# Two expert lists instead of one, and the last stage of 18 images placed between the second lists

## The chip, the core and the metric

The kernel runs on one core of a Trainium2 chip. The core has five engines with an instruction queue each: TensorE (PE, matrix products and transposes, results in PSUM), VectorE (DVE), ScalarE (ACT), GpSimd (POOL, here also the engine that issues gathers and scatters) and SyncE (SP, which issues plain transfers). Each engine works through its queue in order and waits on semaphores for the others. The metric is the device time of one execution in microseconds, the median of several runs; the page and all views come from one profiled execution.

## The reference

Input: 32 images of 128 channels, 56 x 56 pixels, fp32; T = 100352 pixels, called tokens.

```
# layer 0
x   = depthwise_conv_7x7(input) + bias                  # per image and channel
x   = layernorm over the 128 channels of each token
logits = x @ Wg + bg                                    # 8 experts
two best experts per token, softmax over the two -> gates; priority = first gate
per expert: keep the CAP = 15680 tokens of highest priority (ties in token order)
y_e = gelu(x @ W1[e] + b1[e]) @ W2[e] + b2[e]           # 128 -> 512 -> 128
out = input + x + layer_scale * sum of gate * y_e over the kept experts
# layer 1, per image
pooled row and column means (weighted 7:3:1:1 over quarters) -> 1x1 conv to 8 channels
  -> h_swish -> two 1x1 convs -> sigmoids a_h, a_w
out = silu(batchnorm(conv_3x3(out * a_w * a_h)))
```

A token is in two experts' lists at most. What an expert keeps depends on all 32 images, because priorities are compared over all tokens.

## The kernel before

Four stages follow each other.

**Depthwise convolution and layer norm.** Two images at a time (a "pair", 49 columns of 128 tokens), the normalised rows and their gates go to `x_d` in memory, the rows alone to `acc_d`, and the first gate of each chosen token into `prio`, a table of 8 experts by 784 columns that stays on chip.

**Routing.** `Routing.steps(e, idx)` makes expert e's list in some fifty steps. 25 of them search the threshold by bisection: `count` (L411) counts on DVE how many entries of `prio[:, e, :]` lie over a bound and PE adds the counts over partitions (L412); three small DVE operations move the bound. Then ties at the threshold are ranked in token order (`keep`), the kept tokens get places by ten bit steps over 912 columns (L499 to L502), and two one-hot products turn places into row numbers `idx[0]` (for gathers) and `idx[1]` (for scatters). Expert 0's routing runs alone ahead of the experts; the other seven are dealt out as `steps` between the blocks of the experts in front of them.

**Experts.** A list is cut in blocks of 4 tiles of 128 tokens and the blocks in chunks (`CHUNKS`, 4, 7, 7, 7 and 6 blocks). For a block, POOL gathers 4 tiles of rows (L594), PE transposes them (L603), DVE copies them out of PSUM (L605), PE and ACT do the first product and the gelu (L613, L614), PE the second (L621), ACT adds the bias (L623), PE transposes back (L630), DVE multiplies by the gate (L640), and POOL scatters the 4 tiles into `acc_d`, adding in memory (L646). POOL gathers and scatters only blocks that hold tokens; PE, DVE and ACT compute every block of a chunk that holds any:

```
with tc.If(taken > CHUNKS[c] * BLK * P, preferred_fallthrough_block=True) as some:
    if c + 1 < NC_:
        gathers(e, c + 1, parts[e])
    compute(e, c, w, steps[c])
    if c + 1 < NC_:
        chunk(e, c + 1, w, steps)
left = [f for fs in steps[c:] for f in fs]
if left:
    with some.Else():
        for f in left:
            f()
```

So steps that were dealt to chunks that are not taken run by themselves, in the Else branch. In POOL's queue the order is: scatters of chunk c-1, gathers of chunk c+1, scatters of chunk c, and so on; the first chunk of the next expert is gathered ahead.

**Last stage.** After all scatters (a "fence" of small memsets on DVE makes the loads wait for them) the images come pair by pair: the accumulated rows are loaded in sevenths (`cxn`), transposed (`cpt`, L905) and added to the input (L907); PE and DVE pool them (L920 to L943); ACT makes the two sigmoids (L949, L950); DVE multiplies the image by both (L953, L954); POOL and ACT combine rows into six planes `v` of a transformed 3 x 3 convolution (L962 to L972); PE multiplies (L982: 6 planes by 3 taps, for each half of an image), DVE adds the products up (L988 to L992), ACT finishes with silu (L994) and stores. The products of a pair are issued a whole pair later than its gates; `v` has two buffers of a whole image, the products five PSUM buffers.

Instructions are written in program order; a scheduler then orders each engine's queue within a stretch between branches by its own estimate of durations.

Of the kernel before, what the change touches and what calls it, by code (L numbers as in the profile page):

```python
# [32 lines left out]
CHUNKS = (0, 4, 11, 18, 25, -(-ST // BLK))  # L33
NC_ = len(CHUNKS) - 1
CB = 7
RW = C + E
T1 = T + P
KB = 8
VB = 2
# [8 lines left out]
def moe_conv_then_coordatt_kernel(ctx: ExitStack, tc: tile.TileContext, a: dict, out: bass.AP):  # L48
# [12 lines left out]
    acc_d = dram.tile([T + ST * P + P, C], F32, name="acc_d")  # L61
# [101 lines left out]
    with ExitStack() as st:  # L163
# [24 lines left out]
        class Pair:  # L188
# [34 lines left out]
            def gates(self):  # L223
# [17 lines left out]
                nc.sync.dma_start(acc_d[rows, :].rearrange("(p j) c -> p j c", p=P), row[:, :, 0:C])  # L241
# [75 lines left out]
    with ExitStack() as st:  # L317
        rc = st.enter_context(tc.tile_pool(name="rc", bufs=1))
        sp = st.enter_context(tc.tile_pool(name="rts", bufs=2))
        rpp = st.enter_context(tc.tile_pool(name="rtp", bufs=1, space=PSUM))  # L320

        ones = rc.tile([P, P], F32, name="ones")
        nc.gpsimd.memset(ones, 1.0)
        ones_h = rc.tile([P, P], F16, name="ones_h")
        nc.gpsimd.memset(ones_h, 1.0)
        ones_t = rc.tile([P, NT], F16, name="ones_t")
        nc.gpsimd.memset(ones_t, 1.0)
        before = rc.tile([P, P], F32, name="before")
        nc.gpsimd.affine_select(out=before, in_=ones, compare_op=ALU.is_gt, fill=0.0,
                                base=0, pattern=[[1, P]], channel_multiplier=-1)  # L330
        before_h = rc.tile([P, P], F16, name="before_h")
        nc.vector.tensor_copy(before_h, before)
        behind_h = rc.tile([P, P], F16, name="behind_h")
        nc.gpsimd.affine_select(out=before, in_=ones, compare_op=ALU.is_gt, fill=0.0,
                                base=0, pattern=[[-1, P]], channel_multiplier=1)
        nc.vector.tensor_copy(behind_h, before)
        ii = rc.tile([P, ST], I32, name="ii")
        iota_h = rc.tile([P, ST], F32, name="iota_h")
        nc.gpsimd.iota(ii, pattern=[[1, ST]], base=0, channel_multiplier=0)
        nc.vector.tensor_copy(iota_h, ii)  # L340
        kk = rc.tile([P, KB], I32, name="kk")
        iota_k = rc.tile([P, KB], F32, name="iota_k")
        nc.gpsimd.iota(kk, pattern=[[1, KB]], base=0, channel_multiplier=0)
        nc.vector.tensor_copy(iota_k, kk)
        pk = rc.tile([P, KB], F32, name="pk")
        nc.gpsimd.iota(kk, pattern=[[P, KB]], base=0, channel_multiplier=1)
        nc.vector.tensor_copy(pk, kk)
        pcol = pk[:, 0:1]
        spare = rc.tile([P, ST], F32, name="spare")
        nc.vector.tensor_scalar(spare, iota_h, float(P), float(T), ALU.mult, ALU.add)  # L350
        nc.vector.tensor_scalar(spare, spare, pcol, None, ALU.add)
        to_come = rc.tile([1, NC_], F32, name="to_come")
        for c in range(NC_):
            nc.gpsimd.memset(to_come[:, c : c + 1], float(BLK * P * (1 - CHUNKS[c]) - 1))
        most = rc.tile([1, NC_], F32, name="most")
        for c in range(NC_):
            nc.gpsimd.memset(most[:, c : c + 1], float(BLK * P * (CHUNKS[c + 1] - CHUNKS[c] + 1) - 1))
        first = rc.tile([P, 1], F32, name="first")
        nc.vector.tensor_copy(first, spare[:, 0:1])
        shift = rc.tile([P, 1], F32, name="shift")  # L360
        nc.vector.tensor_scalar(shift, pcol, -float(P), None, ALU.add)

        junk = rc.tile([P, NT], F32, name="junk")

        class Routing:

            def __init__(self, n):  # L370
                t = lambda name, shape, dt: rc.tile(list(shape), dt, name=f"{name}_r{n}")
                self.cnt = t("cnt", [P, 1], F32)
                self.mid = t("mid", [P, 1], F32)
                self.enough = t("enough", [P, 1], F32)
                self.thr = t("thr", [P, 1], F32)
                self.room = t("room", [P, 1], F32)
                self.eq = t("eq", [P, NT], F16)
                self.run = t("run", [P, NT], F16)
                self.nth = t("nth", [P, NT], F32)
                self.keep = t("keep", [P, NT], F16)  # L380
                self.gone = t("gone", [P, NT], F16)
                self.n = t("n", [P, 1], F16)
                self.bi = t("bi", [P, 1], I32)
                self.lo = t("lo", [P, 1], I32)
                self.left = t("left", [1, NC_], F32)
                self.room_l = t("room_l", [P, 1], F32)
                self.h0 = t("h0", [P, 1], F32)
                self.v = t("v", [P, KB * P], U16)
                self.bit = t("bit", [P, P + NT], U16)
                self.dist = t("dist", [P, KB * P], F16)  # L390
                self.full = t("full", [P, KB * P], F16)
                self.hk = t("hk", [P, KB], F32)
                self.hot = t("hot", [P, 2, KB, ST], F16)
                self.q = t("q", [P, ST], F32)
                self.qi = t("qi", [P, ST], I32)
                self.a = t("a", [P, ST], F32)
                self.pair = t("pair", [P, ST], F32)
                self.ps = rpp.tile([P, 2, ST], F32, name=f"ps_r{n}")

            def steps(self, e, idx):  # L400

                r, out = self, []
                tot = r.ps[:, 0, 0:1]

                def step(f):
                    out.append(f)

                def count(op, scalar):  # L410
                    nc.vector.tensor_scalar(junk, prio[:, e, :], scalar, None, op, ALU.add, accum_out=r.cnt)  # L411
                    nc.tensor.matmul(tot, lhsT=ones, rhs=r.cnt, start=True, stop=True)  # L412

                for b in range(1, 25):

                    @step
                    def _(b=b):
                        if b == 1:  # L420
                            nc.vector.memset(r.thr, 0.5)
                        else:
                            nc.vector.tensor_scalar(r.enough, tot, float(CAP), 2.0 ** (1 - b), ALU.is_ge, ALU.mult)
                            nc.vector.tensor_tensor(r.thr, r.thr, r.enough, ALU.add)
                        nc.vector.tensor_scalar(r.mid, r.thr, 2.0**-b, None, ALU.add)
                        count(ALU.is_ge, r.mid)


                @step
                def _():  # L430
                    nc.vector.tensor_scalar(r.enough, tot, float(CAP), 2.0**-24, ALU.is_ge, ALU.mult)
                    nc.vector.tensor_tensor(r.thr, r.thr, r.enough, ALU.add)
                    count(ALU.is_gt, r.thr)

                by_pair = r.run.rearrange("p (i j) -> p i j", j=TPP)

                @step  # L440
                def _():
                    nc.vector.tensor_scalar(r.room, tot, -1.0, float(CAP) + 0.5, ALU.mult, ALU.add)
                    nc.vector.tensor_scalar(r.eq, prio[:, e, :], r.thr, None, ALU.is_equal)
                    nc.vector.tensor_tensor_scan(r.run, ones_t, r.eq, 0.0, ALU.mult, ALU.add)


                    pre = r.ps[:, 0, 0:NPAIR]
                    nc.tensor.matmul(pre, lhsT=before_h, rhs=by_pair[:, :, TPP - 1], start=True, stop=False)
                    nc.tensor.matmul(pre[:, 1:NPAIR], lhsT=behind_h, rhs=by_pair[:, 0 : NPAIR - 1, TPP - 1],
                                     start=False, stop=True)  # L450

                @step
                def _():
                    nc.vector.tensor_tensor(r.nth.rearrange("p (i j) -> p i j", j=TPP), by_pair,
                                            bc(r.ps[:, 0, 0:NPAIR].unsqueeze(2), [P, NPAIR, TPP]), ALU.add)

                @step
                def _():
                    nc.vector.scalar_tensor_tensor(r.keep, r.nth, r.room, r.eq, ALU.is_le, ALU.mult)

                @step
                def _():
                    nc.vector.scalar_tensor_tensor(r.keep, prio[:, e, :], r.thr, r.keep, ALU.is_gt, ALU.add)

                @step
                def _():

                    nc.vector.tensor_tensor_scan(r.gone, ones_t, r.keep, 0.0, ALU.add, ALU.subtract)
# [608 lines left out]
```

## Time and profile before

| | us |
|---|---|
| median of 3 runs (4669.65 to 4675.83) | 4672.91 |
| profiled execution | 4676.35 |
| its span, first to last instruction | 4674.5 |
| PE busy | 3662.5 (78%) |
| POOL busy | 2692.2 (58%) |
| DVE busy | 2173.8 (47%) |
| ACT busy | 1314.9 (28%) |

The shares are means over four stages with different limits, so they say little; the stages have to be read one by one. On the page, a group's line shows engine and operation, names and shapes, the number of instructions, busy time and mean duration in ns, then the idle time of that engine just before them and what ended it. "issue" means that nothing the profile shows was waited for. `PEclk` or "granted clock" is the share of TensorE's full clock.

### The profile page before, as it was taken

How to read it: one execution, taken by the hardware profiler on the slowest of the kernel's cores; microseconds unless marked ns; L12 is line 12 of the kernel's file. 1: busy time of each engine (PE TensorE's matmuls, PEld its weight loads, DVE VectorE, ACT ScalarE, POOL GpSimd, SP SyncE). 2: the span in 40 equal slices, each digit the busy share in tenths (PEclk: the TensorE clock that was granted, in tenths of full speed). 3: DMA queues.
4: the chain of work that ended last, by engine and by line, in shares of the span. 5: the costliest groups of instructions: out<-in, count | busy, mean ns of one | idle time of the engine just before them, and what ended most of it. 6: DMA issues, size and time to landing. Idle time of an engine off the chain costs nothing. (4 is left out here: it accounts for less than half of the span.)

```text
span 4674.5 us, 50118 instructions
## 1 busy us (share of the span) xinstructions
PE 3662.5 (78%) x17669; PEld 2031.1 (43%) x17669; DVE 2173.8 (47%) x4727; ACT 1314.9 (28%) x2555; POOL 2692.2 (58%) x1862
## 2 busy tenths in 40 slices
PE   9999989775167667767667756687582999999999
PEld 4444449775133333433333322333231555555555
DVE  1111117988757346654521101111013877787776
ACT  1111117554022222222223322232230333333333
POOL 1001003354068878678778766887785756565655
PEclk9999999877578878878778977888785999999999
DMA  9999987987322333323323332333335344344432
GB/s 155 176 176 176 176 177 255 343 314 275 123 43 37 42 55 36 42 43 40 44 44 43 43 46 44 44 42 42 46 41 126 136 151 151 123 156 151 154 124 74
DMA packets 866353, 526.90 MB, mean 113 GB/s; under 512 B 543880, under 2 KB 835488, under 8 KB 855648
## 3 DMA queue, kind: packets, MB, share of 16 engines
q1 hardware_dynamic: 504848, 327.79, 24.6%
q0 software_dynamic: 118720, 91.19, 14.9%
q10 hardware_dynamic: 242320, 102.85, 9.8%
q8 instruction: 155, 2.54, 0.2%
q14 instruction: 310, 2.54, 0.2%
HBM read 268.72 MB, written 252.97 MB: 112 GB/s over the span
## 5 line engine op out<-in xcount | busy, mean ns | idle before, releaser
L646 POOL DMA_INDIRECT acc_d<-yo,idx x676 | 1074.3, 1589 | 251.1 <-issue 198.7
L614 ACT ACTIVATE ht<-ph,bias 128x512 f32<-128x512 f32 (+1 forms) x700 | 477.9, 683 | 929.8 <-PE ph L613 928.1
L982 PE MATMUL pc<-v,wk 128*128 128x392 f32 x1920 | 696.9, 505 | 3.2 <-POOL v L967 3.2
L613 PE MATMUL ph<-fxt,w 128*128 128x512 f32 (+1 forms) x1400 | 683.1, 631 | 0.0
L137 PE MATMUL acc<-xt,band 56*64 56x424 f32 (+3 forms) x7168 | 668.9, 529 | 2.6 <-DMA xt<-in_x 2.6
L594 POOL DMA_INDIRECT xg_r<-x_d,idx x556 | 546.1, 982 | 175.6 <-issue 139.8
L621 PE MATMUL py<-ht,w 128*128 128x512 f32 (+1 forms) x1400 | 633.5, 596 | 5.8 <-POOL w L666 5.8
L982 PEld LDWEIGHTS pc<-v,wk 128*128 128x128 f32 x1920 | 344.9, 189 | 306.5 <-issue 94.4
L137 PEld LDWEIGHTS acc<-xt,band 56*64 56x64 f32 x7168 | 321.7, 133 | 349.2 <-issue 276.7
L605 DVE COPY fxt<-pt 128x512 f32<-128x512 f32 (+1 forms) x175 | 119.6, 683 | 748.6 <-PE pt L603 684.0
L603 PE MATMUL pt<-ident,xg_r 128*128 128x128 f32 (+1 forms) x568 | 125.6, 326 | 432.9 <-DMA xg_r<-x_d,idx 414.2
L962 POOL TENSOR_TENSOR d<-pad 128x3248 f32<-128x3248 f32 x32 | 228.2, 7132 | 406.4 <-DVE pad L954 406.4
L275 PE MATMUL lnps<-proj,lnyt 128*128 128x136 f32 x1568 | 361.7, 399 | 103.0 <-ACT sq L280 75.0
L275 PEld LDWEIGHTS lnps<-proj,lnyt 128*128 128x128 f32 x1568 | 349.7, 316 | 115.6 <-ACT sq L280 86.5
L125 POOL COPY band<-hk 56x392 f32<-56x392 f32 x128 | 65.3, 510 | 575.5 <-issue 527.5
L613 PEld LDWEIGHTS ph<-fxt,w 128*128 128x128 f32 x1400 | 273.0, 206 | 270.9 <-issue 262.2
L621 PEld LDWEIGHTS py<-ht,w 128*128 128x128 f32 x1400 | 258.4, 193 | 272.4 <-issue 263.9
L150 DVE TENSOR_SCALAR yt<-acc,dwb 128x448 f32<-128x448 f32 x128 | 87.5, 684 | 584.6 <-PE acc L137 337.0
L992 DVE SCALAR_TENSOR_TENSOR y<-pc,y 128x392 f32<-128x392 f32 x640 | 318.4, 557 | 32.3 <-PE pc L982 32.3
L623 ACT ACTIVATE fyt<-py,b 128x512 f32<-128x512 f32 (+1 forms) x175 | 119.6, 683 | 654.8 <-PE py L621 641.9
L603 PEld LDWEIGHTS pt<-ident,xg_r 128*128 128x128 f32 (+1 forms) x568 | 81.5, 163 | 505.9 <-DMA xg_r<-x_d,idx 369.0
L640 DVE TENSOR_TENSOR yo<-pb,xg_r 128x512 f32<-128x512 f32 (+2 forms) x147 | 98.3, 671 | 416.1 <-PE pb L630 363.3
(221 smaller groups left out, 4505.2 us busy)
## 6 DMA issues: line engine op xcount, KB each, us to landing
x_d<-xn SPq DMA_DIRECT2D x16, 3332.0 KB
xt<-in_x SPq DMA_DIRECT2D x128, 392.0 KB
y_d<-yt ACTq DMA_DIRECT2D x256, 196.0 KB
lnyt<-y_d SPq DMA_DIRECT2D x16, 3136.0 KB
acc_d<-xn SPq DMA_DIRECT2D x16, 3136.0 KB
x<-in_x SPq DMA_DIRECT2D x16, 3136.0 KB
cxn<-acc_d SPq DMA_DIRECT2D x112, 448.0 KB
out<-y ACTq DMA_DIRECT2D x64, 784.0 KB
```

The lines of the kernel that those rows point to most:

```text
L137: nc.tensor.matmul(acc[c][half * G : (half + 1) * G, :, lo:hi], lhsT=band[rows, dw, :], rhs=xt[rows, im, lo + s : hi + s], start=(n == 0), ...
L275: nc.tensor.matmul(ps[:, j, :], lhsT=yf[:, self.j0 + g + j, :], rhs=proj, start=True, stop=True)
L594: d = nc.gpsimd.indirect_dma_start(out=xg[0:n, k, :], out_offset=None, in_=x_d[:, :], in_offset=bass.IndirectOffsetOnAxis(ap=idx[0][0:n, t ...
L603: nc.tensor.transpose(pt[:, k * P : k * P + n], xg[0:n, k, 0:C], ident[0:n, 0:n])
L605: nc.vector.tensor_copy(xt[:, 0:N_], pt[:, 0:N_])
L613: nc.tensor.matmul(ph[:, 0:N_], lhsT=w[0][:, f * P : (f + 1) * P], rhs=xt[:, 0:N_], start=True, stop=True)
L614: nc.scalar.activation(ht[:, f, 0:N_], ph[:, 0:N_], AF.Gelu, bias=w[2][:, f : f + 1])
L621: nc.tensor.matmul(py[:, 0:N_], lhsT=w2[:, f, :], rhs=ht[:, f, 0:N_], start=(f == 0), stop=(f == NF - 1))
L646: d = nc.gpsimd.indirect_dma_start(out=acc_d[:, :], out_offset=bass.IndirectOffsetOnAxis(ap=idxs[e][1][0:n, t : t + 1], axis=0), in_=yo[0: ...
L962: nc.gpsimd.tensor_tensor(d, high, low, ALU.subtract)
L982: nc.tensor.matmul(m[k], lhsT=wk[k][:, dw, :], rhs=v[:, k, rows, dw : dw + W], start=(dw == 0), stop=(dw == 2))
L992: nc.vector.scalar_tensor_tensor(r[x], m[k], f, r[y_], ALU.mult, ALU.add)
```

## The change

The images are cut in two groups (`GROUPS`: pairs 0 to 8 and 9 to 15, so 18 and 14 images). Each expert has two lists, one per group; lists 0 to 7 are those of the first group, 8 to 15 those of the second. Each group has its own accumulator. All eight thresholds are searched ahead of everything, on all experts in two halves that take turns; `kept` then marks kept tokens over all 32 images, `listed` makes one group's list from them (at most 441 columns instead of 784). The routing of all 16 lists is dealt out among lists 0 to 7.

The last stage is cut into some twenty pieces per image (`slot`): seven `merge` (load, transpose, add, for 8 rows), `squeeze`, `pooled`, `attend` (sigmoids), `gate`, `combined` (the planes `v`, for half an image), `conv` (one or two planes' products and sums). The pieces of images 0 to 17 are dealt out as `steps` among lists 8 to 15; there `combined` runs on DVE alone. The 14 others follow after the last list, with `combined` on POOL and ACT as before. Buffers change: `xs` and `cx` (loads of 8 rows) have three, `pad` two, `v` one per half image, products two PSUM buffers beside the lists and five afterwards, borrowed from the experts' pools.

The scaling of W2 by the layer scale moves from POOL to DVE, chunks have 4, 6, 6, 6, 6 and 3 blocks, and weights are loaded once per list, so twice per expert.

```diff
-CHUNKS = (0, 4, 11, 18, 25, -(-ST // BLK))
-CB = 7
+CHUNKS = (0, 4, 10, 16, 22, 28, -(-ST // BLK))
+CB = 6
+GROUPS = ((0, 9), (9, NPAIR))
...
-    acc_d = dram.tile([T + ST * P + P, C], F32, name="acc_d")
+    acc_d = [dram.tile([T + ST * P + P, C], F32, name=f"acc{g}_d") for g in range(NG)]
...
+    def count(h, op, bound):
+        es = sides[h]
+        for e in range(es.start, es.stop):
+            nc.vector.tensor_scalar(junk, prio[:, e, :], bound[:, e : e + 1], None, op, ALU.add, accum_out=cnt[:, e : e + 1])
+        nc.tensor.matmul(tots[h], lhsT=ones, rhs=cnt[:, es], start=True, stop=True)
...
+    for b in range(1, 25):
+        for h in range(2):
+            if b > 1:
+                raised(h, 2.0 ** (1 - b))
+            nc.vector.tensor_scalar(mid[:, sides[h]], thr[:, sides[h]], 2.0**-b, None, ALU.add)
+            count(h, ALU.is_ge, mid)
...
-            nc.gpsimd.tensor_tensor(w2, w2, bc(ls_bc.unsqueeze(1), [P, NF, C]), ALU.mult)
+        nc.vector.tensor_tensor(w2, w2, bc(ls_bc.unsqueeze(1), [P, NF, C]), ALU.mult)
...
+    SHARES = (7, 9, 7, 2, 1, 1)
+    PIECES = (56, 48, 40, 40, 40, 40, 40, len(order))
+    for l in range(E):
+        w = one_list(l, w, dealt(some_routing(PIECES[l]), SHARES))
...
+    def merge(n, q):
+        k = (NM * n + q) % 3
+        pt = trp.tile([P, BLK * P], F32, tag="tr", name=f"cpt{n}_{q}")[:, 0 : BLK * MT]
+        for j in range(BLK):
+            nc.tensor.transpose(pt[:, j * MT : (j + 1) * MT], cxs[k][:, j, :], ident[0:MT, 0:MT])
+        nc.vector.scalar_tensor_tensor(pads[n % 2][:, 1 + q * MB : 1 + (q + 1) * MB, 1 : W + 1],
+                                       pt.rearrange("c (r w) -> c r w", w=W), beta_c, xss[k], ALU.add, ALU.add)
+        m = NM * n + q + 3
+        if m // NM in group_of and group_of[m // NM] == group_of[n]:
+            load(m // NM, m % NM)
...
+    def gate(n):
+        img = pads[n % 2][:, 1 : H + 1, 1 : W + 1]
+        nc.vector.tensor_tensor(img, img, bc(aw.unsqueeze(1), [C, H, W]), ALU.mult)
+        nc.vector.tensor_tensor(img, img, bc(ah.unsqueeze(2), [C, H, W]), ALU.mult)
+
+    def combined(n, ch, shared):
...
+        if shared:
+            nc.scalar.mul(t, low[:, :, 1:3, :], 4.0)
+            nc.gpsimd.tensor_tensor(d, high, low, ALU.subtract)
...
+        else:
+            stt = nc.vector.scalar_tensor_tensor
+            stt(t, low[:, :, 1:3, :], -4.0, high[:, :, 1:3, :], ALU.mult, ALU.add)
+            nc.vector.tensor_tensor(d, high, low, ALU.subtract)
+            nc.vector.tensor_tensor(v[:, 1], t[:, :, 1, :], t[:, :, 0, :], ALU.add)
...
+        out_ += [new(merge, n, 0), cv(0, 1, 2), old(combined, n - 1, 1, shared),
+                 new(merge, n, 1), cv(0, 3), new(merge, n, 2), cv(0, 4), new(merge, n, 3), cv(0, 0), cv(0, 5),
+                 new(squeeze, n, 0), new(merge, n, 4), cv(1, 1, 2), new(merge, n, 5), new(merge, n, 6), new(squeeze, n, 1),
+                 cv(1, 3), new(pooled, n), cv(1, 4), new(attend, n), cv(1, 0), cv(1, 5), new(gate, n),
+                 new(combined, n, 0, shared)]
...
+    few = {k: (pcp, "pc") for k in range(6)}
+    many = {1: (pcp, "pc"), 2: (pcp, "pc"), 3: (php, "ph"), 4: (php, "ph"), 0: (pyp, "py"), 5: (pcp, "pc")}
...
+    LSHARES = (8, 10, 6, 1, 1, 1)
+    for g in range(1, NG):
+        pieces = [f for n in range(2 * GROUPS[g - 1][0], 2 * GROUPS[g - 1][1]) for f in slot(n, False, few)]
+        at = [0] + [len(pieces) // (2 * E) + (len(pieces) - len(pieces) // (2 * E)) * e // (E - 1) for e in range(E)]
+        for e in range(E):
+            l = g * E + e
+            steps = dealt(pieces[at[e] : at[e + 1]], LSHARES if e else (0,) + LSHARES[1:])
...
+    scatters(len(lists) - 1, NC_ - 1)
+    fenced(yo_all[0] + yo_all[1])
+    for n in range(2 * GROUPS[-1][0], N + 1):
+        for f in slot(n, True, many):
+            f()
```

## The prediction

> **What bounds the kernel now.** I read the page first, then the stages by windows, then groups by shape, then the timeline where two stages meet. The page's dearest groups:
>
> ```profile
> span 4674.5 us, 50118 instructions
> ...
> L646 POOL DMA_INDIRECT acc_d<-yo,idx x676 | 1074.3, 1589 | 251.1 <-issue 198.7
> ...
> L982 PE MATMUL pc<-v,wk 128*128 128x392 f32 x1920 | 696.9, 505 | 3.2 <-POOL v L967 3.2
> ...
> L594 POOL DMA_INDIRECT xg_r<-x_d,idx x556 | 546.1, 982 | 175.6 <-issue 139.8
> ...
> L962 POOL TENSOR_TENSOR d<-pad 128x3248 f32<-128x3248 f32 x32 | 228.2, 7132 | 406.4 <-DVE pad L954 406.4
> ```
>
> A tile of 128 tokens costs POOL a scatter (1.59 us) and a gather (0.98), each with 0.3 us of issue before it. The scatters' idle is almost all "issue", so POOL waits for nobody there. The windows by stage (us, PE, PEld, DVE, ACT, POOL busy, granted clock, DMA share, GB/s):
>
> ```profile
> 1198.80:1301.90 103.10, 19.98 (x83) 17.28 (x83) 79.33 (x219) 0.00 (x0) 2.55 (x3) 0.50 0.18 62
> 1301.90:3553.00 2251.10, 1547.15 (x4734) 776.38 (x4734) 709.26 (x1783) 598.47 (x876) 1746.27 (x1363) 0.82 0.32 43
> 3553.00:3650.00 97.00, 49.69 (x231) 27.10 (x231) 69.49 (x107) 15.44 (x16) 47.98 (x26) 0.72 0.56 181
> 3650.00:4600.00 950.00, 946.47 (x3663) 500.85 (x3663) 752.89 (x1198) 325.63 (x316) 594.99 (x230) 1.00 0.41 140
> ```
>
> First the routing of expert 0, alone. Then the experts: 676 tile pairs in 2251 us, 3.33 us a pair, POOL the bound, PE idle 700 us. Then a start of 97 us, then the last stage, where PE is 99.6% busy at the full clock: 33.2 us an image (the timeline repeats every 33). Group rows by shape price the DVE parts, the timeline a block of 512 tokens on PE:
>
> ```profile
> L411 DVE TENSOR_SCALAR_CACHE_REDUCE junk<-prio,mid_r 128x784 f32<-128x784 f32 x192 | 196.9, 1025 | 3.8
> ...
> L954 DVE TENSOR_TENSOR pad<-x,ah 128x3136 f32<-128x3136 f32 x32 | 111.8, 3494 | 0.0
> ...
> L953 DVE TENSOR_TENSOR x<-x,aw 128x3136 f32<-128x3136 f32 x32 | 110.4, 3451 | 4.1 <-ACT aw L950 4.1
> ```
>
> ```profile
> 3483.27 3.60 PE L613 MATMUL ph<-fxt,w 128*128 128x512 f32 x8
> 3486.70 0.60 PE L630 MATMUL pb<-ident,fyt 128*128 128x128 f32 x4
> 3487.14 3.60 PE L621 MATMUL py<-ht,w 128*128 128x512 f32 x8
> 3490.57 0.58 PE L603 MATMUL pt<-ident,xg_r 128*128 128x128 f32 x3
> ```
>
> From 3483.27 to 3491.09: 7.82 us a block, undisturbed.
>
> **The work in the lists.** Counting kept tokens with the reference's routing on its inputs, experts 0 to 7 take 31, 15, 25, 31, 2, 4, 31, 31 blocks: 170, or 676 tiles, as the scatters show. PE computes whole chunks: 175. After the cut, images 0 to 17 take 18, 9, 14, 18, 1, 2, 31, 31 (124 blocks, 494 tiles; PE computes 140), the rest 13, 7, 11, 14, 1, 2, 0, 0 (48 blocks, 192 tiles; PE computes 74). Experts 6 and 7 have more tokens of first gate exactly 1.0 than places, and ties go in token order, so all they keep lies in the first 15 images. Two things follow: PE gets 39 blocks more (305 us of PE), and four of the eight second lists leave POOL next to nothing to do while over half of the image work is dealt to them.
>
> **Step 1, thresholds.** 25 counts for 8 experts: 200 on DVE, 1.08 us apart where the timeline has two in a row, plus 50 half steps of three small operations at 0.19 us: 216 + 28 = 244 us. The round over PE (0.76 us) hides behind the other half. Before, only expert 0's 25 rounds of 2.3 us stood here (57). The rest of its routing took 45 us at 784 and 912 columns; at 441 and 569 the ten bit steps shrink from 24 to 15, so 36. First gather at 1199 + 244 + 36 = 1479 instead of 1302. Nothing covers this: all of prio must exist and no list is ready. The 175 counts that leave the expert stage (about 290 us of DVE with their small operations) give nothing back, because DVE is 31% busy there.
>
> **Step 2, first lists.** 494 pairs at 3.33 us: 1645 (at the undisturbed pace of 1.25 + 1.86 us: 1536). Lists 4 and 5 need POOL for 13 and 27 us but carry 40 routing steps each, some 55 us of DVE: 40 us more, between 0 and 80. Gathering list 8's first chunk ahead: 20 us. PE ends 44 us before POOL does, as now (3510 against 3554). PE is free for the second lists at 1479 + 1645 + 40 + 20 - 44 = 3140. The yo memsets, the second accumulator and the scaling moved from POOL to DVE cost nothing here; the DVE's idle time hides them, otherwise 16 times 0.6 us.
>
> **Step 3, second lists beside 18 images.** PE owes 74 x 7.82 = 579 and 18 x 33.2 = 598; POOL owes only 192 x 3.33 = 639. So PE bounds it, and all of the last stage's PE work is still ahead. At the front, the fence memsets on DVE wait for list 7's last scatters; queued behind them are list 8's copies, for which PE waits. Four blocks (31 us) stand before, POOL needs some 44: with the constants' DMAs 25 us (0 to 60). SP now carries the weights behind image loads that wait for merges; they are needed a list later, so nothing, or a landing of 3 to 4 us a list if the loads stand still.
> Where a list ends early, its image pieces run alone. By the shares that is 19/27 of the pieces of lists 12 to 15 and some of the others: 8.3 images. There DVE now does the row combinations too: 24 passes at 0.49 (nine in 4.42 us in the timeline), 7 merges at 0.56 (two of 512 columns take 1.26), squeeze and pooling 3.3, gate 6.9, and 9744 elements at L953's 1.1 ns (10.7): 36.6 us, plus waits for products, 42 an image (33 if PE stayed the bound, 48 with POOL-like waits): 349. The other 9.7 images mix with the blocks: 322 + 579 = 901 us of PE. It works in order, with two PSUM buffers for products, two shared for transposes, one v a half, and products waiting for gate and combinations. I take 90% dense, between the 99.6% of the stage now and the 69% beside POOL: 1001. Sum 349 + 1001 + 25 = 1375, to 4515.
>
> **Step 4, the last 14 images.** Now an image's products run a whole pair behind its gate, so the 7 us gate and POOL's 20 us hide. In the built order of the changed kernel they run right behind: after an image's two sigmoid products come the next image's seven merges, then at once products that need v. In that loop: merges on DVE 2.4 us, gate 3.45, merge 0.6, gate 3.49 (9.9); POOL then d for half an image 3.57, t 1.54, one v 0.89, v1 0.82: the first product starts at 16.7. PE has 5 us of transposes and squeeze to fill that. Then 72 matmuls at 0.328 and the rest, 26 us. Loop 42.7. The same stall costs clock. Rows around an idle stretch of 11.5 us on PE:
>
> ```profile
> 1774.80:1777.10 2.30, 0.00 (x0) 0.00 (x0) 0.00 (x0) 0.68 (x1) 2.00 (x2) 1.00 0.54 54
> 1777.10:1786.30 9.20, 0.07 (x1) 0.07 (x1) 2.78 (x10) 0.00 (x0) 7.67 (x6) 0.50 0.39 34
> 1786.30:1790.70 4.40, 4.40 (x9) 2.23 (x10) 4.37 (x7) 0.91 (x2) 2.39 (x3) 0.50 0.18 17
> ```
>
> After 2.3 us idle the clock halves, and PE works 4.4 us before it returns: 2.2 us lost a stall. So 45 us an image, against 33.2: 14 x 45 = 630, and 46 for the last image's loop, products and store: 676.
> [...]
> [...]
>
> **Sum.** 3140 + 1375 + 676 = 5191, and 1.9 us that the profiled execution has around its span (4676.35 against 4674.5); it lies 3.4 above the median of the runs shown (4672.91): 5190 us, 11% slower. Ends: lists 3050 to 3200, second lists 1240 to 1500, last images 560 to 730. About 0.2% is what a measurement can tell from no change.
>
> **Rivals.** *Dense overlap (faster).* Pieces and blocks fill each other's waits, 33.2 us an image throughout, POOL at its undisturbed 3.11 us: 1479 + 1536 + 20 - 44 = 2991, then 579 + 598 + 465 + 25: 4658, and 4660 with the 1.9 around the span, 0.35% under the profiled execution. For it: a scheduler orders the pieces, and PE is 99.6% dense today. Against it: the built order of step 4. It decides while PE stalls for under 16 us in all, half a microsecond an image; beyond that the change is slower.
> *Loop half hidden.* If the merges and spare banks take most of the stall, 37 us an image last, 38 alone, 96% dense mixed, lists done at 3110: 3110 + 315 + 939 + 25 + 564 = 4953.
> *Cold PE.* If stalls of the mixed part also halve the clock again and again, as the 0.82 of the expert stage shows can be, 72% dense, 48 and 50 us an image, lists at 3170: 3170 + 398 + 1251 + 25 + 750 = 5594.
> *The split is not as counted.* The change may not empty lists 14 and 15: were ties at 1.0 not as in my count, experts 6 and 7 would leave 13 blocks each behind. Then 26 blocks of 13.3 us (346) leave the first lists and PE computes 24 more (188) in the second: near 5030.
>
> **How the numbers follow.** The sum above 64% (own range 5060 to 5330), half hidden 17%, another split 2%, cold 12%, dense 5%. Outside 4930 to 5430 lie most of the dense and cold cases and the low edge of the half hidden one, together under 20%. Faster by over 0.2% only in the dense case, 4%, no change 1%, slower 95%: the PE work behind step 2 alone is 1640 us, against 1121 now, and POOL gives back only 182 pairs.
>
> **What would show it.** Right: first gather near 1479; PE busy over 85% from about 3140 on while POOL falls to half; 42 to 48 us between sigmoids in the last 14 images with granted clock under 1.0. Wrong: a first gather before 1420, an image period under 38 at the end, second lists done within 1250 us, or POOL still dense after 3200.

## The result, and the profile after

The changed kernel takes 5324.56 us (median of 4, 5322.45 to 5325.98) against 4673.63 for the kernel before on the same chip: a ratio of 1.1393, 95% interval 1.1374 to 1.1413. The forecast was 5190 (4930 to 5430), so the sign and the range held; the time is 134 us above the forecast, and most of that sits in one term (step 2 below). The profiled execution has a span of 5320.7 us.

The groups of the page that answer to those shown of before:

```profile
span 5320.7 us, 54751 instructions
...
L662 POOL DMA_INDIRECT acc_d<-yo,idx x686 | 1137.3, 1658 | 600.7 <-issue 245.5
L1009 PE MATMUL pc<-v,wk 128*128 128x392 f32 x2304 | 870.3, 527 | 140.8 <-DVE v L995 67.1
...
L609 POOL DMA_INDIRECT xg_r<-x_d,idx x502 | 494.6, 985 | 254.5 <-issue 107.2
...
L609 POOL DMA_INDIRECT xg_f<-x_d,idx x184 | 192.4, 1046 | 311.8 <-DVE idx L581 235.3
```

686 scatters, as counted (494 + 192), at 1.66 us each against 1.59 for the 676 of before. What changed are the idle columns: the image products (L1009), which waited 3.2 us in the whole kernel before, now have 140.8 us of idle time before them, most of it for their row combinations (67.1 us for those on DVE, 54.9 for those on POOL), and the first gather waits 235.3 us for the thresholds and the first list. The stages by windows (us, PE, PEld, DVE, ACT, POOL busy, granted clock, DMA share, GB/s), cut where the first gather, list 8's first transpose and the end of the images beside the lists lie:

```profile
1198.80:1451.50 252.70, 33.73 (x129) 28.73 (x129) 248.83 (x644) 0.00 (x0) 5.70 (x13) 0.50 0.06 20
1451.50:3217.00 1765.50, 1248.88 (x3595) 571.55 (x3596) 514.93 (x1401) 480.35 (x701) 1300.48 (x1016) 0.83 0.29 42
3217.00:4626.00 1409.00, 1186.79 (x4135) 596.58 (x4133) 760.82 (x1217) 432.89 (x551) 546.95 (x403) 0.92 0.35 83
4626.00:5320.70 694.70, 549.93 (x1920) 286.19 (x1920) 376.65 (x632) 173.40 (x204) 313.81 (x232) 0.85 0.31 99
```

Row one is DVE alone (98% busy). Row two is POOL's stage, as in the kernel before. In row three PE is 84% busy and POOL falls to 39%: PE owes image work and blocks, and POOL is done with little. In row four nobody is the bound: PE 79%, DVE 54%, POOL 45%, and the clock at 0.85 where it was 1.00 before. That is the mark of a loop of waits. One of its periods, from the timeline, PE first, then DVE and POOL:

```profile
4855.37 0.38 PE L963 MATMUL pa<-z_t,wwt 8*128 8x56 f32 x2
...
4862.69 0.57 PE L929 MATMUL cpt<-ident,cx 112*128 112x112 f32 x4 [2.81 <-DMA cx<-acc_d]
...
4872.90 18.91 PE L1009 MATMUL pc<-v,wk 128*128 128x392 f32 x48 [3.12 <-POOL v L985]
...
4901.58 0.38 PE L963 MATMUL pa<-z_t,wwt 8*128 8x56 f32 x2
```

```profile
4858.37 3.42 DVE L969 TENSOR_TENSOR pad<-pad,aw 128x3136 f32<-128x3136 f32 x1
...
4862.30 3.42 DVE L970 TENSOR_TENSOR pad<-pad,ah 128x3136 f32<-128x3136 f32 x1
```

```profile
4865.86 3.65 POOL L981 TENSOR_TENSOR d_t<-pad 128x1624 f32<-128x1624 f32 x1 [24.57 <-DVE pad L970]
4869.44 1.64 POOL L984 TENSOR_TENSOR t_t<-pad,t_t 128x812 f32<-128x812 f32 x1
```

From one image's sigmoid product to the next it is 46.2 us, in every period. After the sigmoid come the gate (two passes of 3.42 us with merges between), then POOL's d and t, and only then the first product: 17.1 us after the sigmoid product's end, and PE has only transposes and squeeze products for that time, some 8 us of work. PE's waits in the last images, from 4640 to 5275:

```profile
PE cpt L929 <- DMA cx<-acc_d: 56.3, 29, 3.2
PE pc L1009 <- POOL v L985: 40.2, 13, 3.1
```

(us in total, times, longest.) More is put down to the image loads than to the combinations, but the waits for loads lie within those 17.1 us, in which DVE goes on from the merges to the gate and POOL from d to v without a pause, so the loads do not set when the products start. The clock in this stretch (same columns as in the stages):

```profile
4862.00:4864.00 2.00, 1.31 (x6) 0.53 (x6) 2.00 (x2) 0.00 (x0) 0.00 (x0) 1.00 1.04 410
4864.00:4866.00 2.00, 0.12 (x2) 0.10 (x2) 2.00 (x2) 0.19 (x1) 0.14 (x1) 0.56 1.08 343
...
4876.00:4878.00 2.00, 2.00 (x4) 1.01 (x4) 0.00 (x0) 0.00 (x0) 2.00 (x2) 0.53 0.00 0
4878.00:4880.00 2.00, 2.00 (x7) 1.13 (x6) 0.00 (x0) 0.00 (x0) 2.00 (x2) 1.00 0.00 0
```

It halves near 4864 and returns near 4878. The products that start at 4872.90 run at half rate for 5.0 us of that, 2.5 us lost in this period. Over the 13 periods the products begin with 2.9 to 6.0 us at half rate, 4.4 in the mean: 2.2 us lost a period, as forecast.

### The profile page after: what moved, and what is told of

It is laid out like the page before. It is cut to its first block, busy times and chain, and to the rows that moved or that the text cites. A ratio compares the mean times of both kernels' runs of the same rounds, so it can differ in the third digit from the quotient of the medians.

```text
span 5320.7 us, 54751 instructions
## 1 busy us (share of the span) xinstructions
PE 4046.4 (76%) x18517; PEld 2152.9 (40%) x18517; DVE 2424.3 (46%) x5246; ACT 1443.3 (27%) x2785; POOL 2439.1 (46%) x1894
## 5 line engine op out<-in xcount | busy, mean ns | idle before, releaser
L662 POOL DMA_INDIRECT acc_d<-yo,idx x686 | 1137.3, 1658 | 600.7 <-issue 245.5
L1009 PE MATMUL pc<-v,wk 128*128 128x392 f32 x2304 | 870.3, 527 | 140.8 <-DVE v L995 67.1
L628 PE MATMUL ph<-fxt,w 128*128 128x512 f32 (+1 forms) x1712 | 868.9, 641 | 114.9 <-DVE fxt L620 109.5
L629 ACT ACTIVATE ht<-ph,bias 128x512 f32<-128x512 f32 (+1 forms) x856 | 585.0, 686 | 1100.4 <-PE ph L628 1089.2
L637 PE MATMUL py<-ht,w 128*128 128x512 f32 (+1 forms) x1712 | 769.1, 591 | 0.0
L1009 PEld LDWEIGHTS pc<-v,wk 128*128 128x128 f32 x2304 | 449.4, 202 | 516.5 <-issue 133.3
L637 PEld LDWEIGHTS py<-ht,w 128*128 128x128 f32 x1712 | 311.8, 190 | 324.7 <-issue 323.8
L618 PE MATMUL pt<-ident,xg_r 128*128 128x128 f32 x598 | 129.3, 328 | 327.3 <-DMA xg_r<-x_d,idx 318.8
L609 POOL DMA_INDIRECT xg_f<-x_d,idx x184 | 192.4, 1046 | 311.8 <-DVE idx L581 235.3
L981 POOL TENSOR_TENSOR d_t<-pad 128x1624 f32<-128x1624 f32 x29 | 105.2, 3628 | 356.1 <-DVE pad L970 351.7
```

Source lines behind the costliest of these rows:

```text
L609: nc.gpsimd.indirect_dma_start(out=xg[0:n, k, :], out_offset=None, in_=x_d[:, :], in_offset=bass.IndirectOffsetOnAxis(ap=idxs[l][0][0:n, t ...
L618: nc.tensor.transpose(pt[:, k * P : k * P + n], xg[0:n, k, 0:C], ident[0:n, 0:n])
L628: nc.tensor.matmul(ph[:, 0:N_], lhsT=w[0][:, f * P : (f + 1) * P], rhs=xt[:, 0:N_], start=True, stop=True)
L629: nc.scalar.activation(ht[:, f, 0:N_], ph[:, 0:N_], AF.Gelu, bias=w[2][:, f : f + 1])
L637: nc.tensor.matmul(py[:, 0:N_], lhsT=w2[:, f, :], rhs=ht[:, f, 0:N_], start=(f == 0), stop=(f == NF - 1))
L662: d = nc.gpsimd.indirect_dma_start(out=acc_d[g][:, :], out_offset=bass.IndirectOffsetOnAxis(ap=idxs[l][1][0:n, t : t + 1], axis=0), in_=yo ...
```

## The experiments

The runs went to different chips. Where the kernel before takes 4673 to 4675 us I call the chip kind A (two chips, and that of the result), where it takes 4741 to 4743 kind B (three). Ratios are against the kernel before on the same chip; between the kinds I compare stretches of the trace only. The times expected in runs 2 to 5 were reckoned from traces of kind A, and those runs went to kind B, so they are read by differences on that chip.

**My theory**: the time comes from three things, thresholds in front of the first gather, a last stage whose order makes PE wait in each image, and the split itself, which puts PE's image work behind POOL's long lists where only 192 of 686 tile pairs are left to hide it. **Rivals** stand with each run.

**1. The changed kernel again** (kind A).

> The changed kernel itself once more, so that the kernels with one part altered are compared with it on the same chip: 1.139 of the kernel before by every theory.

5322.4 us, 1.1387 (1.1368 to 1.1406). This is what the other kind A runs are held against.

**2. Thresholds alone** (kind B). The kernel of before, with the search of the changed kernel ahead of everything and 25 steps less in each expert's routing:

```
-                for b in range(1, 25):            # 25 steps of each expert's routing
-                    ...
+        for b in range(1, 25):                    # ahead of the first list, all eight
+            for h in range(2):
+                if b > 1: raised(h, 2.0 ** (1 - b))
+                ...; count(h, ALU.is_ge, mid)
-        PIECES = (16, 32, 32, 24, 16), (16, 32, 28, 16, 8)
+        PIECES = (8, 16, 16, 12, 8), (8, 16, 14, 8, 4)
```

> The kernel of before with one part of the change alone: all eight thresholds are searched ahead of the first list, the rest as it was. My theory: the 218 us that the search took in the changed kernel plus some 45 of listing stand in front of the first gather, where 103 stood, and the 175 counts that leave the expert stage give nothing back, since DVE was 31% busy there: first gather near 1462, time 4674 + 160 = 4834 (4810 to 4850). Rival: the counts also took time from POOL's lists while they ran beside them, so the expert stage shortens from 2251 to under 2180 and the time ends under 4770.

4864.64 against 4742.62: +122 us, 1.0264 (1.0232 to 1.0296). The first gather moved from 1301.9 (the kernel before on kind A) to 1456.6 us, 155 later as expected, yet the total grew by 122 only: some 33 us came back. So "the counts give nothing back" is wrong by 33 us, and the rival is wrong in size. Where they came back is open, for there is no trace of the kernel before from that chip; it is not the last stage, whose 31 periods take 1017 us here and 1016 in the kernel before on kind A.

**3. One list per expert** (kind B, same chip). The split undone, the rest of the change kept:

```
-GROUPS = ((0, 9), (9, NPAIR))
+GROUPS = ((0, NPAIR),)
```

> The changed kernel with one list per expert for all 32 images (one entry in the table of groups): thresholds ahead, chunks and the new last stage stay, the second lists and the overlap go. My theory: the overlap only just pays for what the split adds, because the last stage's 32 images cost 46.2 us each here as the last 14 did: first gather 1461, PE free near 3670, some 50 us of start, 32 x 46.2 + 47: 5245 (5180 to 5310), so the split is worth between -60 and +140 us. Rival: the split is what hides 18 images and without it the time is 18 x 33 us or more longer than the changed kernel's, over 5600.

5257.55 us, 1.1081 (1.1045 to 1.1117). The time lies in the range, but with luck: the range was reckoned for kind A, where the same ratio would give 5179, just under it. The rival falls: without the overlap the kernel is faster. Its last stage runs at 46.2 to 46.5 us an image in all but the first two periods, where run 2, with the old order of the last stage, has 33.0 to 33.3 in most. That is 32 x 13 = 416 us, and the two runs lie 393 apart. The split's own price is read against run 4, the changed kernel but for the fence, on the same chip: 205 us. That is above my range of -60 to 140. Run 4 can stand for the changed kernel there: from list 0's first transpose to list 15's it takes 3169 us, and run 5, which has the fence on DVE, 3167.

**4. The fence on POOL** (kind B, same chip).

```
-        fences.append([nc.vector.memset(t[:, :, 0:1], 0.0).ins for t in tiles])
+        fences.append([nc.gpsimd.memset(t[:, :, 0:1], 0.0).ins for t in tiles])
```

> The changed kernel with the twelve fence memsets on POOL in place of DVE, so that list 8's copies are no longer queued behind list 7's last scatters. My theory: the PE wait of up to 70.6 us at the start of list 8 goes, 40 to 75 us less: 5265 (5245 to 5285). Rival: the first images can't be loaded before list 7's scatters either way, so the work comes late by the same amount and the time stays within 20 us of 5325.

5462.59 us, 1.1523 (1.1488 to 1.1558). List 8 lasts 253.7 us from its first transpose to list 9's; in run 5, on the same chip with the fence on DVE, 251.2, and PE's longest wait for list 8's copies is 45.1 us against 45.4. Nothing gained, but the wait did not go either, so this run does not say what it costs. The waits of DVE at list 8 say why it stayed:

```profile
DVE w1t L871 <- DMA acc_d<-yo,idx: 44.1, 1, 44.1
```

The memset of `w1t`, one of the last stage's constants, waits for the same scatters as the fence did. Its pool takes the memory that the routing's pool gave back, with list 7's indices in it, which is the likely reason. The fence had a twin.

**5. A later order in the last 13 images** (kind B, same chip). Merges and squeezes of an image ahead, more products of the image before behind its sigmoid:

```
+        out_ = [new(merge, n, 0), ..., new(merge, n, 3), new(squeeze, n, 0),
+                cv(0, 1, 2), old(combined, n - 1, 1, True), new(merge, n, 4), ..., new(merge, n, 6),
+                new(squeeze, n, 1), cv(0, 3), new(pooled, n), cv(0, 4), new(attend, n), cv(0, 0), cv(0, 5),
+                new(gate, n), cv(1, 1, 2), new(combined, n, 0, True), cv(1, 3), cv(1, 4), cv(1, 0), cv(1, 5)]
```

> The changed kernel with another order in the last 13 images alone: an image's merges and both squeezes go ahead, and all of the image before's second half (18 products) and two products of its first half run between the gate and the products that need it. My theory: the 46.2 us a period are a wait of PE for gate and row combinations, so it falls to 34 to 37 us and the clock rises: 5325 - 13 x 10 = 5190 (5160 to 5215). Rival: the period is held by something that the order doesn't touch (POOL's 20 us, DVE, the transposes' clock, the image loads): it stays over 43 us and the time over 5280.

5386.77 us, 1.1359 (1.1324 to 1.1393), 76 us less than run 4. The period falls from 46.2 to 41.0 us in the mean (38.1 to 42.9), the clock in those images rises from 0.85 to 0.92. So the order matters, but I missed the size. PE still waits 5.7 us a period for the row combinations (us in total, times, longest):

```profile
PE pc L1009 <- POOL v L985: 74.5, 13, 7.5
```

Eight products behind the sigmoid are not enough for gate and combinations.

**6. Products half an image later** (kind A, with run 1). Three v buffers, so that combinations are made half a slot before their products; the gate in two halves; chunks of 5 blocks to make room:

```
-    vs = [cp1.tile([C, 6, RP, W + 2], F32, name=f"v{k}") for k in range(2)]
+    vs = [cp1.tile([C, 6, RP, W + 2], F32, name=f"v{k}") for k in range(3)]
-        v, pad = vs[ch], pads[n % 2]
+        v, pad = vs[(2 * n + ch) % 3], pads[n % 2]
-        out_ += [new(merge, n, 0), cv(0, 1, 2), old(combined, n - 1, 1, shared), ...,
-                 new(gate, n), new(combined, n, 0, shared)]
+        cv = lambda d, ch, *ks: (lambda: conv(n - d, ch, ks, banks)) if d <= n < N + d else None
+        out_ += [new(merge, n, 0), cv(2, 1, 1, 2), new(merge, n, 1), cv(2, 1, 3), ..., new(merge, n, 4), cv(1, 0, 1, 2),
+                 new(merge, n, 5), new(merge, n, 6), ..., new(attend, n), cv(1, 0, 0), new(gate, n, 0), cv(1, 0, 5),
+                 new(combined, n, 0, shared), new(gate, n, 1), new(combined, n, 1, shared)]
-CHUNKS = (0, 4, 10, 16, 22, 28, ...)
+CHUNKS = (0, 4, 9, 14, 19, 24, 29, ...)
```

> The changed kernel with products half an image later: three v buffers in place of two, so that the combinations of an image have half a slot of products between them and their use, the gate in two halves, chunks of 5 blocks in place of 6 to make room for the third buffer. My theory: the wait of PE for gate and combinations goes altogether, 33.5 to 36 us an image in the last 14 (150 us less), and 20 to 60 us less beside the second lists: 1.10 of the kernel before (1.09 to 1.11). Rival: the clock or the transposes hold the period, it stays over 40 us: 1.125 or more.

5167.45 us, 1.1060 (1.1041 to 1.1078): 155 us less than run 1. The period is 38.4 us in the mean (37.9 to 39.5), not 33.5 to 36; that is 101 of the 155 us, and which of the edits gave the other 54 is not separated. The wait for combinations is gone; another has come, 3.6 us in each image:

```profile
PE pa L942 <- DVE pad L932: 47.0, 13, 3.6
```

A merge on DVE stands behind two passes that need ACT's copy `odd`, and that copy stands in ACT's queue behind scalings that wait for POOL's d (ACT's timeline):

```profile
4664.93 0.54 ACT L985 ACTIVATE v<-d_t 128x406 f32<-128x406 f32 x1 [7.23 <-POOL d_t L984]
4665.50 0.88 ACT L986 ACTIVATE d_t<-d_t 128x812 f32<-128x812 f32 x1
4666.29 0.47 ACT L1021 COPY odd<-pc 128x392 f32<-128x392 f32 x1
```

So ACT's wait for POOL, 7.23 us here and ahead of the copy in its queue, reaches PE as 3.6 us.

**7. The groups in the other order** (kind A, same chip). The last 14 images' lists first, their last stage beside the 494 pairs of the first 18 images:

```
-GROUPS = ((0, 9), (9, NPAIR))
+GROUPS = ((9, NPAIR), (0, 9))      # and images taken in that order in the last stage
```

> The changed kernel with the two groups in the other order: the first lists serve the last 14 images, the second lists the first 18, and the 14 images' last stage runs beside the second lists. My theory: the split came out dear because the lists that hide the image work held only 192 of 686 tile pairs; with 494 pairs behind, POOL is the bound there and the images fill PE's gaps: first lists end near 2330, second lists near 4200 to 4250, then 18 x 46.2 + 47 = 879: 5100, which is 1.09 of the kernel before (1.075 to 1.11). Rival: PE works in order and stalls in every piece, so image work adds to the lists wherever it lies: 1.13 or more.

5136.4 us, 1.0982 (1.0964 to 1.1001): 186 us less than run 1, within the range, and the rival falls. The stages:

```profile
1451.50:2405.00 953.50, 668.24 (x2015) 312.86 (x2016) 421.31 (x1272) 255.55 (x371) 558.36 (x443) 0.83 0.25 36
2405.00:4250.00 1845.00, 1601.91 (x5192) 780.67 (x5192) 706.95 (x1131) 637.82 (x857) 1283.15 (x969) 0.93 0.40 75
```

The second lists now keep PE 87% and POOL 70% busy at once; in the changed kernel's POOL had 39%. The first lists end 75 us later than I said: 192 pairs took 953.5 us.

**8. All of it, cut at image 14** (kind A, same chip).

```
+GROUPS = ((7, NPAIR), (0, 7))      # with run 6's buffers and order
+        at = [len(pieces) * sum(blocks[:e]) // sum(blocks) ...]       # pieces by a list's blocks
+PIECES = (90, 50, 75, 85, 10, 10, 4, ...)                             # routing to the first four lists
```

> All of it together: the groups in the other order and cut at image 14, so that the last 18 images run beside the second lists (110 blocks), products half an image later with three v buffers, pieces dealt by the blocks of each list, routing dealt to the first four lists. My theory: first gather 1451, first lists to 2450, second lists 1520 to 1680 to 4190, then 14 x 34.5 + 60: 4730, 1.012 of the kernel before (0.98 to 1.04). Rival: PE's stalls and the in-order queues keep the mixed part 20% above the bound of either engine: 1.07 or more.

4808.61 us, 1.0279 (1.0257 to 1.0301): 514 us less than run 1 and inside the range, at its slow side. The last images keep 38.4 us.

**9. The fence behind list 8's first chunk** (kind B, another chip). The memsets and the constants' DVE operations bound by a dependency behind the chunk's last `yo`:

```
+                after(d.ins, anchor[E], why="the copies of the first second list go ahead")
```

> The changed kernel with the fence memsets, and the constants' DVE operations that stood beside them, bound behind the last product of list 8's first chunk, so that that chunk's copies go ahead of them on DVE. My theory: of the 70.6 us that PE waits there some 31 are then filled with the four blocks that are already gathered; the rest (list 7's last scatters, until 3286 us) stays: 30 us less, 1.132 of the kernel before (1.129 to 1.136). Rival, suggested by the fence on POOL: the wait only moves, 1.137 to 1.141.

5469.39 us, 1.1517 (1.1465 to 1.1569). The waits of PE in the first 168 us of list 8, of run 1 (kind A), of run 5 (kind B, the fence as in the changed kernel) and of this one:

```profile
PE ph L628 <- DVE fxt L620: 70.9, 2, 70.6
```

```profile
PE ph L628 <- DVE fxt L620: 45.8, 2, 45.4
PE ph L628 <- ACT ht L629: 11.7, 2, 10.3
```

```profile
PE ph L628 <- DVE fxt L620: 42.5, 2, 36.5
PE ph L628 <- ACT ht L629: 28.3, 6, 11.2
```

Against run 1 the wait is 28 us shorter, but most of that is the kind of chip: against run 5 the longest wait fell by 9 us, the waits for ACT grew by 17, and list 8 lasts 260.5 us, not less than run 5's 251.2 (247.9 in run 1). The rival has it right: the wait moves. POOL's timeline suggests why the list gains nothing: in the changed kernel's trace POOL is at list 7's scatters and list 8's gathers until 3284, 67 us into the list, and list 8's 52 scatters at 1.86 us, 12 more gathers and list 9's first 16 at 1.25 follow, so it owes 199 of the 248 us whatever PE does. The other 49 are not explained by this sum; for 22 of them (3286 to 3308) POOL itself has next to nothing to do and in the end waits for list 8's first products.

**10. Seven thresholds beside list 0** (kind B, same chip as run 9). Run 8 with only expert 0's search ahead, the fence as in run 9, and the next image's last merges ahead of the first product pair:

```
+    for f in searched(slice(0, 1), sums[0][:, 0, 0:1]): f()
     ready[0] = len(order)
+    for fs in zip(*(searched(es, r.ps[:, 0, 0 : es.stop - es.start]) for es, r in zip(sides, sets))):
+        order += fs                       # 26 rounds of experts 1 to 3 and 4 to 7
```

> The groups in the other order, cut at image 14, products half an image later, pieces dealt by blocks, as in the run of that name, and three things more: only expert 0's threshold is searched ahead, the other seven in steps beside list 0; the fence and the constants behind list 8's first chunk; the next image's last merges ahead of the first product pair. My theory: list 0 starts 150 us earlier and grows by 35 (115 less), 3.6 us less an image in the last 14 (50 less), 30 less at list 8: 4808 - 195 = 4613, 0.987 of the kernel before (0.965 to 1.005). Rival: the counts on DVE hold up list 0's copies and routing as long as they did alone, so the 150 us come back: 1.01 or more.

4958.78 us, 1.0451 (1.0415 to 1.0486), a miss. List 0 starts at 1307.3 instead of 1473.5, but its time to list 1 grows from 244.3 to 347.0, and list 8 starts only 24 us earlier than in run 8 (2474.4 against 2498.7). The chip is of the other kind, so that 24 may be too low; still, most of the 150 us came back, as the rival had it. Run 11, which has the same search and the kind of chip of run 8, bears this out: its list 8 starts 84 us earlier than run 8's (2414.5), and 47 of the 84 are its four short lists.

**11. First chunks of 2 blocks** (kind A). Run 10 without the moved fence, and the lower half's combination half a slot later, so that no ACT copy stands behind it:

```
-CHUNKS = (0, 4, 9, 14, 19, 24, 29, ...)
+CHUNKS = (0, 2, 7, 12, 17, 22, 27, ...)
+        second = (lambda: combined(n - 1, 1, shared)) if 1 <= n <= N else None     # after cv(1, 0, 1, 2)
```

> The groups in the other order and cut at image 14, products half an image later, seven thresholds beside list 0 (the fence and the constants as in the changed kernel), and two things more: first chunks of 2 blocks in place of 4, and the combination of an image's lower half half a slot later, so that no ACT copy or Silu stands behind a scaling that waits for POOL. My theory: against 1.028 of the kernel before, 60 us less by the earlier start, 15 to 20 us less for each of the six lists of 0 to 3 blocks (100), 4 us less an image in the last 14 (60): 4808 - 220 = 4590, 0.98 of the kernel before (0.965 to 1.00). Rival: with 2 blocks ahead PE waits for gathers at the start of each list and the gain is eaten: 1.01 to 1.04.

4704.16 us against 4674.3: 1.0055 (1.0040 to 1.0070), between the theory's range and the rival's. The lists of 0 to 3 blocks take 28 to 43 us (42 to 54 in run 8) and the last images 36.4 us. No version here beats the kernel before; this one comes to within 30 us.

**12. The fence ahead of list 8's gathers** (kind B, a third chip). Run 11 with this, and with an image's pooling and sigmoids one product later.

```
             scatters(l - 1, NC_ - 1)
+        if between:
+            between()
         rows_for(l, 1)
         gathers(l, 1)
```

> The kernel of the run before (first chunks of 2 blocks, 1.0055 of the kernel before) with two orders changed: the fence stands right behind list 7's last scatters, ahead of list 8's gathers, and an image's pooling and sigmoids stand one product later each. My theory: of the 62.5 us that PE waits at list 8 for copies behind the fence some 40 go, since no gather stands ahead of the fence any more and list 7 is empty; 3.2 us less an image in the last 14 (40 us): 4625, 0.989 of the kernel before (0.98 to 1.0). Rival, as the two earlier moves of the fence had it: the wait at list 8 is POOL's backlog under another name and stays, and only the 40 us of the last images come: 0.997.

4945.11 us, 1.0436 (1.0410 to 1.0462); run 11 has no counterpart on such a chip, so the ratio decides nothing. The trace says more: PE's wait for list 8's copies is 63.0 us, as in run 11 (63.0, on the other kind), and the last images take 38.7 us (36.4 in run 11). Neither of the two gains came; three moves of the fence (runs 4, 9, 12) have left most of the wait where it was.

## Why the prediction was right, step by step

**The three parts.** On one chip (runs 2, 3, 4): thresholds 122 us, the last stage's new order 393 (with the other small parts of the change in it), the split 205, together the 720 us between the kernel before and run 4. On kind A the whole is 651, and it was not taken apart there. The second number is the largest, and the forecast's step 4 is its core; but it stands for all 32 images in the new loop, and the changed kernel has 14 there, some 14 x 13 = 182 us.

**Step 1, thresholds: right, a little dear.** 252.7 us to the first gather against 280 forecast. The counts cost what the timeline of before said; the term that was too large is the 28 us for the half steps' small operations, which cost next to nothing. From DVE's timeline:

```profile
1302.30 1.03 DVE L402 TENSOR_SCALAR_CACHE_REDUCE junk<-prio,mid 128x784 f32<-128x784 f32 x1
...
1303.37 1.03 DVE L402 TENSOR_SCALAR_CACHE_REDUCE junk<-prio,mid 128x784 f32<-128x784 f32 x1
...
1304.33 0.15 DVE L407 TENSOR_SCALAR enough<-ps_r 128x4 f32<-128x4 f32 x1
1304.44 1.03 DVE L402 TENSOR_SCALAR_CACHE_REDUCE junk<-prio,mid 128x784 f32<-128x784 f32 x1
```

Two counts start 1.07 us apart whether a small operation stands between them or not.

**Step 2, first lists: the mis-sized term.** PE was free at 3217, not 3140; from the first gather it took 1765 us, not 1661. I priced the lists by the pair (3.33), but that price carried each list's own cost with it. Held against POOL's undisturbed 3.11 us a pair, the first lists leave over 2251 - 2102 = 149 us at 676 pairs (before), 1765 - 1536 = 229 at 494 (changed) and 953 - 597 = 356 at 192 (run 7). The fewer pairs, the more is left over. Lists 4 and 5, with 1 and 2 blocks, took 64 and 65 us in the changed kernel, where I had given the two 80 in all: in list 4 PE is 38 us at the first chunk's four blocks, and the other 26 go to routing steps that have no products beside them. Lists 0 to 3, with 59 blocks, took 866 us, 80 more than 3.33 a pair gives; lists 6 and 7, with 62, took 756, 63 less. So no price by the pair alone meets this, nor a fixed price for each list on top, since the same eight lists leave 149, 229 and 356; short lists need a price of their own.

**Step 3: right in sum, wrong in a cause.** 1409 us against 1375, PE 84% busy where I had over 85. That the sum is so near is partly luck: the wait behind the fence is 70.6 us (forecast 25, 0 to 60), and the five image periods here in which PE computes no block take 43 to 56 us, 48 in the mean (forecast 42), so the mixed part must have come out cheaper than I had it. What the wait costs is not shown: runs 4, 9 and 12 moved the fence, but the longest wait was 45.1, 36.5 and 62.7 us with the move against 45.4, 45.4 and 62.5 without (the last pair from two kinds of chip), and the list got no shorter. POOL's backlog of 199 us speaks for a wait that hides another engine's debt, but that is argued.

**Step 4, the last 14 images: right.** 46.2 us a period against 45, 694 in all against 676, clock 0.85. The first product comes 17.1 us after the sigmoid product (16.7 forecast), and from there to the next sigmoid product it is 29.1 us (28.2). Runs 5 and 6 put more work between an image's sigmoid and the products that need it, and the period followed: 41.0, 38.4, then 36.4 in run 11. That the order makes the period is shown. That it would fall at once to 34 was wrong each time: behind each wait taken away stood a shorter one (v, 5.7 us an image in run 5; ACT's copy, 3.6 in run 6; the pooling's chain, 3.2 in run 11).

**The rivals.** *Dense overlap* needed stalls under half a microsecond an image; 13 us were there. *Half hidden* needed 37 us an image: only after a third buffer and a new order did the kernel come near that. *Cold PE* fell with the mixed part's clock of 0.92. *Another split* fell with the last scatter, which ends at 4256.9 while lists 14 and 15 begin at 4356 and 4499: they are empty, as counted.

**The clock.** In the kernel before, the clock halves 2.3 us into an idle stretch of 11.5 us on PE (the prediction's rows). In the changed kernel it halves near 4864.2, some 1.5 us after the end of an idle gap of 2.81 us on PE. In the next period PE's work ends at 4906.1, and the clock halves near 4908.6, 2.5 us into a gap of 2.73 us (columns as in the stages):

```profile
4905.50:4908.50 3.00, 0.61 (x5) 0.39 (x4) 3.00 (x2) 0.02 (x1) 0.00 (x0) 1.00 0.87 254
4908.50:4909.00 0.50, 0.16 (x1) 0.19 (x2) 0.50 (x2) 0.00 (x0) 0.00 (x0) 0.61 1.07 365
```

So in these two periods it halved with gaps of 2.7 and 2.8 us; what sets the moment the runs do not show.

## What to carry to other kernels

Work that is to be hidden belongs beside the stage with the most spare time on the engine it needs: the same split, in the other order, was worth 186 us here. Count in the built order how much independent work stands in an engine's queue between a step and its user, and compare that with the chain's length; half an image of lag, bought with one more buffer and smaller chunks, was worth 155. Before you cost a wait, ask whether the engine behind it is idle or in debt, and before you compare a wait between two runs, whether they ran on the same kind of chip. Price short lists apart from long ones.

## What was not expected of the hardware

The chips differ by 1.5% on the kernel before, and by 2.6% between the changed kernel on kind A (run 1) and run 4 on kind B. The difference lies in the lists: the first eight take 1822 us in run 4 and 1749 in run 1, from there to list 15's start it is 1346 and 1286, while the last images take 46.2 us each on both. It isn't in the indirect DMAs, whose scatters take 1653 ns in run 4 and 1658 in the changed kernel on kind A. Waits of ACT go with it, here in the first lists of run 4:

```profile
ACT ht L629 <- remote: 232.2, 34, 38.2
ACT fyt L639 <- remote: 121.2, 9, 19.0
```

The same stretch of run 1 has no such row, nor have runs 8 and 11, on kind A. All runs on kind B looked at have them (run 12: 148.2 and 136.4 us up to 4400), and lists 6 and 7 together take 787 us there (run 4) against 756 (run 1). What releases ACT in these waits the traces don't tell.
